# Latents in a decoder kernel: the first four tiles' roots, scaling and turns move between the projections

## The chip, the cores and the metric

The kernel runs on one core of a Trainium2 chip. The metric is device time in microseconds (us), the median of several executions. A core has five engines that run side by side, each through its own list of instructions: TensorE (PE; its weight loads are listed as PEld), VectorE (DVE), ScalarE (ACT), GpSimd (POOL) and SyncE (SP, which only issues transfers here). TensorE writes its results to PSUM, from where VectorE or ScalarE takes ("evicts") them to on-chip memory.

## What is computed

The program is two layers of a decoder on x of shape (4, 1024, 256): attention, cross attention and a feed-forward block in each. The change is in the fifth of the six blocks, the cross attention of the second layer, in which the 1024 rows of x are the latents and a context of 77 rows is attended to together with them. All arithmetic is float32. Cut to what matters:

```python
def _L1_xattn_ref(x, latents, mask, ...):          # x: context (4, 77, 256), latents (4, 1024, 256)
    def rmsnorm(x, gamma):
        n = jnp.linalg.norm(x, axis=-1, keepdims=True) * x.shape[-1] ** (-0.5)
        return x / jnp.maximum(n, RMS_EPS) * gamma
    xn = layernorm(x, ln_x_g, ln_x_b)
    ln = layernorm(latents, ln_l_g, ln_l_b)
    q = ln @ W_q
    kv = jnp.concatenate([xn @ W_kv, ln @ W_kv], axis=1)
    k, v = (kv[..., :INNER], kv[..., INNER:])      # 4 heads of 64
    q, k, v = (to_heads(q), to_heads(k), to_heads(v))
    qn = rmsnorm(q, q_gamma) * SCALE
    kn = rmsnorm(k, k_gamma)
    sim = jnp.einsum('bhid,bhjd->bhij', qn, kn)
    attn = softmax(where(mask, sim, -max))
    out = jnp.einsum('bhij,bhjd->bhid', attn, v)
    return out @ W_out + b_out                     # added to the latents
```

## The kernel before

The class `Latents` works through the four batches one after the other. A batch has 1024 rows: 8 tiles (`NTB`) of 128 rows. Its preparation is a generator, `projected(b, got)` (from line 2005), that stops at each `yield`; what lies between two yields is called a piece here.

In the first eight pieces, one for each tile t, TensorE makes `pk` (keys and values, 512 columns, line 2020) and `pq` (queries, 256 columns, line 2022). ScalarE copies the keys to `k` and the queries to `q` and squares both into `sq` (lines 2024, 2025, 2027, 2028). VectorE copies the values to `v` (line 2026) and sums the squares of each head into `sums[:, t]` (line 2029). `q` lies in a buffer that the trace calls `xn`.

The ninth piece takes the reciprocal root of all 64 sums of a partition: `inverse_rms` (line 1960, then `rsqrt`, lines 86 to 94), thirteen VectorE instructions in a chain: a scaling, three that make a first guess, and three Newton rounds of three. The queries' half is copied to `rq` (line 2040), which later scales the scores. Pieces ten and eleven scale four tiles of keys in place (`times_rms`, line 1967) and turn four tiles of queries; pieces twelve and thirteen turn the keys. To turn four tiles (`turn`) is eight transposes on TensorE (line 2047), four to a PSUM tile, and two evictions of 128x512 by ScalarE (line 2048) into `qT` or `kT`, with gamma as the scale. After that a fourteenth call ends the generator.

All of this takes its PSUM tiles from one pool, `ps_t`, with two buffers of the name `pt`, used in turn: a matmul into a `pt` waits until the tile two before it has been evicted by all its readers. The attention's transposes and projections use the same two buffers. The scores have three buffers of their own (`sc0`, `sc1`, `sx`).

In this stage the order of instructions on TensorE, ScalarE and VectorE is the order in which the program writes them (`manual_schedule`).

Batch 0 is prepared before any attention: its pieces alternate with those of the context (`of_context`), which has a reciprocal root of its own for 16 sums (issued after the fifth piece, in the first round of the loop over `range(12)`), a scaling of its keys (after the seventh piece) and four small turns of its keys (lines 1998 and 2001, issued after pieces ten to thirteen).

Batches 1 to 3 are prepared during the attention of the batch before. A batch's attention has 16 steps: four pairs of row tiles, times two pairs of heads, times two tiles. A step makes scores for two heads (`scores`, line 2072 and following; `nm` and `nx` are their maxima on VectorE), takes the exponentials on ScalarE (lines 2099 and 2105), turns the step before's weights (`turned`, lines 2122 and 2129), does pieces of earlier weighing and output work (`weighed`, `project_out`), and then calls `next(coming)` once. `coming` is `ahead(b + 1, got)`: at its k-th call it does piece k + 1 of `projected(b + 1)`, and from k = 9 on also a piece of `rows(b + 2)`, the layer norm and turning of the batch after next (statistics, root and normalization on VectorE, transposes on TensorE). For batch 1 the rows come first, so that its pieces start in the fourth step of batch 0's attention, with two calls at k = 12; its rows' pieces are doubled from k = 11 on.

## Time and profile before

| what | value |
|---|---|
| median of 3 runs | 4187.01 us (4185.9 to 4192.95) |
| the profiled execution's own time | 4175.77 us |
| its span, first to last instruction | 4174.0 us |
| mean granted TensorE clock | 0.977 |

The span is what the profile shows of one execution, and the execution's own time is 1.8 us longer. The changed block runs from about 2858 us to 3562 us of the span. In parts, with the busy time of each engine:

| from, to (us) | what runs | PE | DVE | ACT | clock |
|---|---|---|---|---|---|
| 2856 to 2872 | batch 0 and context prepared | 14.28 | 5.31 | 4.87 | 1.00 |
| 2872 to 2885 | the same | 11.22 | 7.64 | 5.64 | 1.00 |
| 2885 to 2902 | the same, to the first scores | 13.50 | 8.72 | 10.22 | 0.84 |
| 2902 to 3060 | attention of batch 0, batch 1 prepared | 142.63 | 105.82 | 83.05 | 0.95 |
| 3060 to 3225 | about batch 1 | 147.72 | 104.04 | 84.58 | 0.98 |
| 3225 to 3395 | about batch 2 | 152.67 | 100.11 | 88.19 | 0.97 |
| 3395 to 3565 | about batch 3, and the next block's statistics | 155.21 | 123.75 | 82.92 | 1.00 |

Lines of a timeline give start, length, engine, line of the kernel, operation, what is written and read, the shape and the count; in brackets stands the time for which the engine was idle before it, and what released it. Matmuls are merged into runs, and their ends are modelled. A row of the windows gives the stretch, its length, the busy time of the engines with the number of instructions, the granted clock (1.00 is full), the share of the transfer engines and GB/s.

### The profile page before, as it was taken

How to read it: one execution, taken by the hardware profiler on the slowest of the kernel's cores; microseconds unless marked ns; L12 is line 12 of the kernel's file. 1: busy time of each engine (PE TensorE's matmuls, PEld its weight loads, DVE VectorE, ACT ScalarE, POOL GpSimd, SP SyncE). 2: the span in 40 equal slices, each digit the busy share in tenths (PEclk: the TensorE clock that was granted, in tenths of full speed). 3: DMA queues.
4: the chain of work that ended last, by engine and by line, in shares of the span. 5: the costliest groups of instructions: out<-in, count | busy, mean ns of one | idle time of the engine just before them, and what ended most of it. 6: DMA issues, size and time to landing. Idle time of an engine off the chain costs nothing.

```text
span 4174.0 us, 58034 instructions
## 1 busy us (share of the span) xinstructions
PE 3933.5 (94%) x22350; PEld 2831.1 (68%) x22350; DVE 2967.8 (71%) x5464; ACT 1629.3 (39%) x2616; POOL 1018.8 (24%) x1218
## 2 busy tenths in 40 slices
PE   8899668999999999999999999998989899899999
PEld 6644336888788887888878877884555555557765
DVE  6646688888878888788878888875567567543324
ACT  4334465334333443333433333433555455112220
POOL 1100001333333343333333333331000000012215
PEclk9989889999999999999999999998999999899999
DMA  2010000000000000000000000000000000302213
GB/s 68 1 41 1 1 23 1 1 1 1 1 1 1 1 1 1 1 1 1 1 1 1 1 1 1 1 1 28 1 1 1 1 1 11 115 25 63 65 41 110
DMA packets 50906, 64.30 MB, mean 15 GB/s; under 512 B 8557, under 2 KB 44769, under 8 KB 50625
## 3 DMA queue, kind: packets, MB, share of 16 engines
q1 hardware_dynamic: 44145, 42.81, 3.2%
q0 software_dynamic: 6480, 17.70, 1.5%
q8 instruction: 181, 2.97, 0.3%
q14 instruction: 100, 0.82, 0.1%
HBM read 42.80 MB, written 17.69 MB: 14 GB/s over the span
## 4 chain that ended last, share of the span: by engine, by line
PE 68%; DVE 15%; ACT 1%; issue 1%; ACTq 0%; DVEq 0%
PE sc L1578 35%; PE po L1607 5%; PE ph L2652 4%; PE ph L2580 3%; PE sc L2072 3%; DVE mx L1586 3%; DVE nm L2085 3%; DVE pr L1596 3%; PE po L2154 2%; PE po L2682 2%; PE po L2567 2%; PE pt L2020 1%; DVE prT L2123 1%; PE pt L2122 1%; DVE km L1568 1%
## 5 line engine op out<-in xcount | busy, mean ns | idle before, releaser
L1578 PE MATMUL sc<-qT,km 128*128 128x256 f32 x8064 | 1789.8, 381 | 8.8 <-DVE pr L1596 8.8
L1578 PEld LDWEIGHTS sc<-qT,km 128*128 128x128 f32 x8064 | 1518.6, 190 | 272.3 <-issue 60.9
L1599 ACT ACTIVATE pr<-pr,zb 128x1024 f32<-128x1024 f32 x512 | 588.2, 1149 | 1316.8 <-DVE pr L1596 1302.1
L1588 POOL PARTITION_ALL_REDUCE top<-mx x512 | 544.6, 1064 | 1449.7 <-DVE mx L1586 1449.7
L1586 DVE TENSOR_REDUCE mx<-sc 128x256 f32<-128x1024 f32 x512 | 625.7, 1222 | 309.2 <-PE sc L1578 306.5
L1596 DVE TENSOR_TENSOR pr<-sc,top 128x1024 f32<-128x1024 f32 x512 | 622.0, 1215 | 0.0
L1568 DVE SCALAR_TENSOR_TENSOR km<-kT,w_L_attn_conv_w,km 128x512 f32<-128x512 f32 x504 | 380.9, 759 | 24.7 <-ACT km L1555 20.0
L1591 POOL COPY tops<-top 32x256 f32<-32x256 f32 x512 | 269.3, 526 | 32.7
L1607 PE MATMUL po<-pr,v 128*32 128x256 f32 x4096 | 249.3, 384 | 0.0
L2085 DVE TENSOR_REDUCE nm<-sc 128x1 f32<-128x1024 f32 x128 | 156.2, 1220 | 79.4 <-PE sc L2072 79.4
L2099 ACT ACTIVATE pr<-sc,nb,rq 128x1024 f32<-128x1024 f32 x128 | 155.1, 1212 | 127.9 <-PE pt L2129 109.5
L1607 PEld LDWEIGHTS po<-pr,v 128*32 128x32 f32 x4096 | 120.4, 110 | 109.6 <-issue 43.2
L2652 PE MATMUL ph<-wgu,xnT 128*128 x568 | 179.8, 459 | 0.6 <-ACT xnT L2641 0.6
L1555 ACT ACTIVATE km<-kT,w_L_attn_conv_w 128x512 f32<-128x512 f32 x252 | 173.5, 706 | 5.4 <-PE po L1361 5.4
L2659 DVE TENSOR_TENSOR xnT<-ph,xnT 128x352 f32<-128x352 f32 x71 | 37.3, 525 | 187.7 <-ACT xnT L2658 187.7
L2137 POOL COPY rb<-rinv 128x256 f32<-128x256 f32 x32 | 12.8, 400 | 629.3 <-DVE rinv L2113 388.3
L2122 PE MATMUL pt<-ident,pr 128*128 128x128 f32 x1024 | 144.4, 282 | 20.4 <-DVE X L2173 11.2
L2122 PEld LDWEIGHTS pt<-ident,pr 128*128 128x128 f32 x1024 | 113.0, 143 | 45.6 <-issue 18.8
L2072 PE MATMUL sc<-kT,qT 64*128 64x512 f32 x512 | 135.0, 627 | 2.9 <-ACT pr L2099 2.9
L2652 PEld LDWEIGHTS ph<-wgu,xnT 128*128 128x128 f32 x568 | 102.3, 190 | 46.0 <-ACT xnT L2641 0.9
L2154 PE MATMUL po<-prT,v 128*64 128x256 f32 x1024 | 132.6, 391 | 0.2 <-DVE oT L2161 0.2
L2123 ACT COPY prT<-pt 128x512 f32<-128x512 f32 x128 | 69.0, 589 | 146.1 <-PE pt L2122 146.1
(515 smaller groups left out, 4845.9 us busy)
## 6 DMA issues: line engine op xcount, KB each, us to landing
yrows<-xnT SPq DMA_DIRECT2D x71, 128.0 KB, 1.7
X<-in_x SPq DMA_DIRECT2D x8, 512.0 KB, 7.3
out<-X SPq DMA_DIRECT2D x8, 512.0 KB, 3.1
wgu<-in_L_ffn_w_gate SPq DMA_DIRECT2D x8, 352.0 KB, 6.6
wgu<-in_L_ffn_w_up SPq DMA_DIRECT2D x8, 352.0 KB
raw<-in_L_ffn_w1T SPq DMA_DIRECT2D x4, 512.0 KB, 3.5
raw<-in_L_ffn_w2T SPq DMA_DIRECT2D x4, 512.0 KB, 3.8
xrows<-xn SPq DMA_DIRECT2D x2, 1024.0 KB, 5.1
```

Source lines behind the costliest of these rows:

```text
L1568: nc.vector.scalar_tensor_tensor(km, keys, weight, km, ALU.mult, ALU.add)
L1578: nc.tensor.matmul(sc[:, j, :], km[:, c, bass.ts(j, P)], qT[:, c, bass.ts(i, Q2)], start=(c == 0), stop=(c == 1),)
L1586: nc.vector.tensor_reduce(mx, sc.rearrange("p j q -> p q j"), AX.X, ALU.max)
L1588: nc.gpsimd.partition_all_reduce(top, mx, P, bass_isa.ReduceOp.max)
L1591: nc.gpsimd.tensor_copy(tops[n][rows, i % (NQ, 2)[n], :], top[rows])
L1596: nc.vector.tensor_tensor(pr, sc, top.unsqueeze(1).to_broadcast([P, KT, Q2]), ALU.subtract)
L1599: nc.scalar.activation(pr, pr, AF.Exp, bias=zb[:, h : h + 1])
L1607: nc.tensor.matmul(po[32 * e : 32 * e + 32, :], v[:, n * KT + j, 4 * g + e, :], prs[e][:, j, :], start=(j == 0), stop=(j == KT - 1),)
L2072: nc.tensor.matmul(sc[e][:, bass.ts(n, 512)], lhsT[at], kT[at, d, bass.ts(n, 512)], start=True, stop=True,)
L2085: nc.vector.tensor_reduce(nm, sc[e], AX.X, ALU.max, negate=True)
L2122: nc.tensor.transpose(pt[:, n, :], pr[e][:, bass.ts(j + n, P)], net.ident)
L2652: nc.tensor.matmul(ph[:, k, :F], s["xT"][:, c, :], wgu[:, bass.ds(s["e"] * GU + (2 * c + k) * F, F)], start=(c == 0), stop=(c == 1),)
```

## The change

`inverse_rms`, the copy to `rq` and the scaling of the keys are put into a function `finish(t)` that does them for four tiles; it is called once for tiles 0 to 3 and once for tiles 4 to 7. `turn` stays as it was and is defined earlier. Inside the loop over the tiles, the first `finish` stands before the projection of tile 5, the turn of the first four tiles' queries before that of tile 6, and the turn of their keys before that of tile 7. After the loop come `finish()` for the last four tiles, the turn of their queries and the turn of their keys, a piece each. The generator has eleven pieces before its end where it had thirteen. Nothing else changes: the calls in `ahead` and in the loop over `range(12)` stay, with the last of them finding nothing to do.

```diff
                 qT = p2.tile([P, 2, S], F32, name="qT")
                 kT = p2.tile([P, 2, S], F32, name="kT")
+                rq = p2.tile([P, NTB, H], F32, name="rq")
+
+                def turn(src, dst, t, g):
...
+                def finish(t=4):
+
+                    flat = sums[:, t : t + 4].rearrange("p t s h -> p (t s h)")
+                    r = inverse_rms(flat, P, 4 * 2 * H, "rs").rearrange(
+                        "p (t s h) -> p t s h", s=2, h=H
+                    )
+                    nc.vector.tensor_copy(rq[:, t : t + 4], r[:, :, 0, :])
+                    times_rms(k[:, t : t + 4], r[:, :, 1, :], P)
+
                 for t in range(NTB):
+                    if t == 5:
+                        finish(0)
+                    if t == 6:
+                        turn(q, qT, 0, gq)
+                    if t == 7:
+                        turn(k, kT, 0, gk)
                     pk = ps_t.tile([P, 512], F32, name="pt")
                     pq = ps_t.tile([P, 512], F32, name="pt")
...
                     yield
-                flat = sums.rearrange("p t s h -> p (t s h)")
-                r = inverse_rms(flat, P, NTB * 2 * H, "rs").rearrange(
-                    "p (t s h) -> p t s h", s=2, h=H
-                )
-                rq = p2.tile([P, NTB, H], F32, name="rq")
-                nc.vector.tensor_copy(rq, r[:, :, 0, :])
+                finish()
                 yield
-
-                def turn(src, dst, t, g):
...
-                for t in range(0, NTB, 4):
-                    times_rms(k[:, t : t + 4], r[:, t : t + 4, 1, :], P)
-                    turn(q, qT, t, gq)
-                    yield
-                for t in range(0, NTB, 4):
-                    turn(k, kT, t, gk)
-                    yield
+                turn(q, qT, 4, gq)
+                yield
+                turn(k, kT, 4, gk)
+                yield
                 got.append((qT, kT, v, rq))
```

More of the change, by code (lines that the diff above doesn't have):

```diff
@@ L2014, in projected @@
                 kT = p2.tile([P, 2, S], F32, name="kT")
-                for t in range(NTB):
+                rq = p2.tile([P, NTB, H], F32, name="rq")
+                def turn(src, dst, t, g):
+                    for d in range(2):
+                        pt = ps_t.tile([P, 4, P], F32, name="pt")
+                        for j in range(4):
+                            nc.tensor.transpose(pt[:, j, :], src[:, t + j, bass.ts(d, P)], net.ident)
+                        nc.scalar.activation(
+                            dst[:, d, t * P : (t + 4) * P], pt.rearrange("p j q -> p (j q)"),
+                            AF.Copy, scale=g,
+                        )
[3 more added lines that the diff above has]
+                        "p (t s h) -> p t s h", s=2, h=H
+                    )
+                    nc.vector.tensor_copy(rq[:, t : t + 4], r[:, :, 0, :])
+                    times_rms(k[:, t : t + 4], r[:, :, 1, :], P)
+                for t in range(NTB):
+                    if t == 5:
[4 more added lines that the diff above has]
+                        turn(k, kT, 0, gk)
                     pk = ps_t.tile([P, 512], F32, name="pt")
@@ L2034, in projected @@
                     yield
-                flat = sums.rearrange("p t s h -> p (t s h)")
-                r = inverse_rms(flat, P, NTB * 2 * H, "rs").rearrange(
-                    "p (t s h) -> p t s h", s=2, h=H
-                )
-                rq = p2.tile([P, NTB, H], F32, name="rq")
-                nc.vector.tensor_copy(rq, r[:, :, 0, :])
-                yield
-                def turn(src, dst, t, g):
-                    for d in range(2):
-                        pt = ps_t.tile([P, 4, P], F32, name="pt")
-                        for j in range(4):
-                            nc.tensor.transpose(pt[:, j, :], src[:, t + j, bass.ts(d, P)], net.ident)
-                        nc.scalar.activation(
-                            dst[:, d, t * P : (t + 4) * P], pt.rearrange("p j q -> p (j q)"),
-                            AF.Copy, scale=g,
-                        )
-                for t in range(0, NTB, 4):
-                    times_rms(k[:, t : t + 4], r[:, t : t + 4, 1, :], P)
-                    turn(q, qT, t, gq)
-                    yield
-                for t in range(0, NTB, 4):
-                    turn(k, kT, t, gk)
-                    yield
+                finish()
+                yield
+                turn(q, qT, 4, gq)
+                yield
+                turn(k, kT, 4, gk)
+                yield
                 got.append((qT, kT, v, rq))
```

## The prediction

> **What bounds the kernel now.** I began with the page's busy shares and its chain of waits. They say that the whole span leans on TensorE, and that the changed stage (lines 2020 to 2173) is a small part of it.

> ```profile
> PE 3933.5 (94%) x22350; PEld 2831.1 (68%) x22350; DVE 2967.8 (71%) x5464; ACT 1629.3 (39%) x2616; POOL 1018.8 (24%) x1218
> ...
> PE 68%; DVE 15%; ACT 1%; issue 1%; ACTq 0%; DVEq 0%
> ```

> Next the timeline of the stage's start (columns: start, length, engine, line, operation, count, idle before it and its releaser). From 2858 to 2901 us batch 0 is projected while no attention runs yet, so no other work covers a wait. The lines are the place where the context's reciprocal root runs, and the end of this prologue:

> ```profile
> 2881.33 0.69 DVE L2029 TENSOR_REDUCE sums<-sq 128x8 f32<-128x512 f32 x1 [0.44 <-ACT sq L2028]
> ...
> 2881.93 0.16 DVE L1960 TENSOR_SCALAR ss_c<-ss_c 77x16 f32<-77x16 f32 x1
> ...
> 2884.27 0.41 DVE L2026 COPY v<-pt 128x256 f32<-128x256 f32 x1
> ...
> 2884.54 1.98 PE L2020 MATMUL pt<-w_L_xattn_W_kv,xnT 128*128 128x512 f32 x4 [0.75 <-ACT sq L2028]
> ...
> 2890.93 1.09 PE L2047 MATMUL pt<-ident,xn 128*128 128x128 f32 x8 [0.35 <-DVE v L2026]
> ...
> 2892.03 0.20 DVE L1960 TENSOR_SCALAR sums<-sums 128x64 f32<-128x64 f32 x1
> ...
> 2895.06 0.18 DVE L2040 COPY rq<-ri_rs 128x32 f32<-128x32 f32 x1
> 2895.15 2.35 DVE L1967 TENSOR_TENSOR k<-k,ri_rs 128x1024 f32<-128x1024 f32 x2
> ...
> 2896.51 1.82 PE L2047 MATMUL pt<-ident,k 128*128 128x128 f32 x8 [1.79 <-DVE k L1967]
> ```

> The reader is to see three things. VectorE does its instructions in the written order: the copy of `v` for tile 5 stands behind thirteen small instructions of the context's root and starts only at 2884.27, though its projection was done before. TensorE, which has two PSUM buffers `pt`, waits for that copy's buffer. And the turns of `k` wait for the root and the scaling (1.79 us).

> Then the granted clock in stretches of 2 us, and one attention step of batch 1:

> ```profile
> 2894.00:2896.00 2.00, 0.65 (x5) 0.26 (x3) 1.85 (x6) 1.67 (x4) 0.00 (x0) 1.00 0.01 4
> 2896.00:2898.00 2.00, 1.49 (x8) 1.44 (x8) 1.50 (x2) 0.48 (x1) 0.00 (x0) 0.67 0.00 0
> 2898.00:2900.00 2.00, 1.67 (x8) 1.18 (x7) 0.00 (x0) 1.55 (x4) 0.00 (x0) 0.50 0.00 0
> ```
> ```profile
> 3147.89 0.42 DVE L2026 COPY v<-pt 128x256 f32<-128x256 f32 x1 [1.98 <-ACT sq L2025]
> ...
> 3149.98 1.22 DVE L2085 TENSOR_REDUCE nm<-sc 128x1 f32<-128x1024 f32 x1 [0.53 <-PE sc L2072]
> ```

> Column nine of the first fence is the clock: it falls to 0.50 after the wait. In the second, VectorE has 1.98 us free before `v` in this step. The stage's windows are PE-busy 90 to 91%: a step is TensorE's work plus under 1 us of waits.

> **The change, part by part.** Counts: the root (13 VectorE instructions) and the copy to `rq` now run twice a batch, so 14 more small VectorE instructions a batch; scalings, turns and their evictions stay as many. No DMA and nothing on POOL or SP is added. The generator has 12 pieces instead of 14.

> *Length of one `finish`.* The thirteen take 2.34 us at 16 elements (2881.93 to 2884.27) and 3.03 at 64 (2892.03 to 2895.06). 32 elements are not in the trace; linear between the two gives 2.57. With 0.09 to the scaling (2895.06 to 2895.15) and half of 2.35 for four tiles, one `finish` is 3.84 us; bounds 3.6 and 4.3 with either end.

> *Prologue.* `finish(0)` is written ahead of tile 5's projection, so it lands between the context's root and the copy of `v` for tile 5: that copy moves from 2884.27 to about 2888.1. Queued behind it are `sums` of tile 5 and all later VectorE work; TensorE's next instruction, now the turn of `q`, needs the buffer. Nothing covers it: **+3.84**. TensorE, not queued behind other work, then idles from 2883.8, the end of tile 5's projection, to 2888.4, 4.6 us. The two turns set between projections cost what one cost before, 1.43 us each (from 2890.93 to 2892.36, when the next user of a `pt` started after ScalarE's eviction): **+2.86**; at 1.09 each if evictions hid, 2.2. At the end only one turn of each kind is left. Before, from the first turn of `q` to the first scores 10.52 us passed (2890.93 to 2901.45). After: 1.10 to the root's start, 3.84 for `finish(4)`, 0.18 to TensorE (k's first scaling ends 2896.33, TensorE starts 2896.51), then 2.34 from the second turn of `k` to the scores as now (2899.11 to 2901.45), and two context turns that used to lie in waits and now come behind it, 0.79 each by ScalarE's eviction of one: 9.04. **−1.5**. The end keeps a root of its own: 32 elements take nearly as long as 64, and 3.84 us stay between the last sum and `k`. Lastly the clock. After 1.79 us of wait it was 0.67, 0.50, 0.50 and 0.63 in four stretches of 2 us, a loss of up to 3.4 us, and eight transposes took 1.82 instead of 1.09. After 4.6 us I expect the same; part of it falls into eviction waits. From 0 to 3.4, I take **+1.0**, nearer to the 0.73 of the eight transposes than to the whole dip. Prologue: 3.84 + 2.86 − 1.5 + 1.0 = **+6.2**; bounds 3.5 (3.6 + 2.2 − 1.5 − 0.8 for `k` at full clock) and 9.1.

> [...]

> *Attention steps.* One `nx` reduction (line 2087) marks each step. Bare periods, read in the last batch, go 7.75, 8.23, 8.61, 9.50 in turn; a projection adds 2.6 to 2.8, a turn alone 0.86 to 1.17, the old root 0 to 0.35. For batch 2's pieces: (a) `finish(0)` with 1.98 us free ahead of `v`: from 3145.83 it ends 3149.7, then `v` and `sums`, so `nm` starts 0.75 late, and the addition to X that TensorE waits for later in the step (0.53) with it: +0.75. (b) The turn of `q` ahead of tile 6's projection: TensorE gets there at 3155.70, ScalarE's exponentials end at 3156.84, its eviction takes 0.69, so the projection starts 1.9 late instead of 1.0. (c) The turn of `k` ahead of tile 7: at 3166.55, ScalarE free at 3167.03, 1.4. (d) `finish(4)`: 0.2, since the root's 0.26 us of slack before `nm` goes. (e) the second turns, beside statistics of the next rows: 1.16 (1.66 before; the scaling that delayed `nm` by 0.5 is gone) and 1.02. After 6.4, before 1.66 + 1.02 + 0.86 + 1.02 = 4.6: **+1.8**. Batch 3, without next rows, by the same pieces with 1.0 for each second turn: 6.25 against 4.07 (1.17 + 1.01 + 0.87 + 1.02), **+2.2**. Batch 1, whose pieces start at the fourth step: `finish(0)` has 4.06 us free, 0; turns 1.7 and 1.9; `finish(4)` 1.15 (0.35 before); second turns 1.02 and 1.16; then a step bound by VectorE's rows 1.34 and, without its turn, 3.4: 11.7 against 8.9 (0.35 + 1.02 + 1.66 + 1.34 + 4.54), **+2.8**. Stage: **+6.8**. Bounds: −1.0 if the eviction waits and the late `nm` are absorbed and only the 0.5s remain, +10.5 at 3.5 a batch (where a held `v` also holds the next step's turns).

> *Sum:* 6.2 + 6.8 = **+13.0 us**, 0.31%. The profiled execution's own time is 4175.8 (span 4174.0 and 1.8 around it), so 4188.8 for a like one; it lay 11.2 below the median of the runs, 4187.0, from which the forecast is **4200.0**.

> **Rivals.** *Only the prologue pays.* TensorE is idle about 9% in the steps, and the four turns' work is the same; if their waits vanish in this slack, +5.3 (without the clock) to +6.2 is left: 4192.7. Against it: a turn alone already costs its whole 1.0 in every kind of step. *Faster: the clock stays up.* Place: 2896 to 2935, where the clock was low in three dips worth 3.4, 5.1 (2906 to 2918) and 1.8 us. If VectorE took `v` ahead of `finish(0)` there is no hold: 2.86 − 1.5 = +1.4, and with first scores reached without a cold start, up to −10.2, and −0.5 twice in the steps: about −10, 4177. It decides from the point where TensorE never waits over 1.8 us between tile 5 and the scores. Against it: the context's thirteen went ahead of `v` in just this way, and `finish(4)` leaves a wait of about 3 us before `k`. *Worse: the hold repeats.* If the late `v` holds TensorE in every batch as in the prologue, 9.1 + 10.5 = +19.6: 4206.6. For: `v` frees one of only two buffers. Against: scores, which need none, come between.

> **How the numbers follow.** Forecast 0.62 (its own range 4195.5 to 4205), only the prologue 0.18, faster 0.12, the hold repeats 0.08. Time: the likeliest, 4200.0. Range: lowest sum 3.5 − 1.0 = +2.5 less the 1.1 by which a run lay under the median, 4188; highest 4206.6 and some of the 5.9 that a run lay above it, 4210. Within 0.2% (8.4 us, about what a measurement of this kernel can tell from no change) lie the second case and a little of the first: 0.20. Faster is the third, 0.12; slower the rest, 0.68.

> **What would show it.** Right: two thirteens of 32 elements per batch; the copy of `v` for tile 5 of batch 0 about 4 us after its projection, and TensorE idle 4 to 5 us before its first `q` turn; first scores about 6 us later after the stage's start; steps with turn and projection 1.4 to 1.9 longer than with projection alone. Wrong: `v` before the small instructions, or a gap between first scores and last step that stays at its length; then the stage's 6.8 falls, and a full clock from 2900 on would turn the sign.

## The result and the profile after

Before 4190.6 us, after 4205.6 us (medians of nine runs each): a ratio of 1.0038, interval 1.0029 to 1.0046, so 12 to 19 us slower. The forecast was 13.0 us more, and 4200.0 us in a range of 4188 to 4210. Measured again (run e11 below) the ratio was 1.0037 (1.0023 to 1.0052).

The spans of the two profiled executions are 4174.0 and 4201.8 us, 27.8 apart and thus further than the medians; of this, 11.6 us lie between tile 5's projection in batch 0 and the end of the attention, as worked out below. The page of the changed kernel, engines and chain of waits:

```profile
span 4201.8 us, 58077 instructions
...
PE 3947.6 (94%) x22338; PEld 2835.9 (67%) x22350; DVE 2975.1 (71%) x5520; ACT 1628.0 (39%) x2616; POOL 1018.8 (24%) x1218
...
PE 67%; DVE 15%; ACT 2%; issue 1%; another core or an unknown queue 0%; ACTq 0%; DVEq 0%
```

VectorE has 56 instructions more (5464 before), four batches of 14, and is busy 7 us longer. ScalarE, GpSimd and the weight loads count as before; 12 matmul records fewer stand beside as many weight loads, so they are missing from the trace and not from the work. TensorE still sets the end. So the page tells nothing of where the time went; the timeline does. First the prologue of the changed kernel. The projection of tile 5 starts at 2885.76 here (2880.95 before); line 2021 is a turn's transposes, 2022 its eviction, 2047 and 2049 the projections, 2053 the copy of `v`:

```profile
2888.91 0.39 ACT L2055 ACTIVATE sq<-pt 128x256 f32<-128x256 f32 x1
...
2889.08 0.17 DVE L1960 TENSOR_SCALAR sums<-sums 128x32 f32<-128x32 f32 x1
...
2889.35 0.66 PE L2021 MATMUL pt<-ident,xn 128*128 128x128 f32 x4 [0.75 <-ACT sq L2055]
...
2890.05 0.69 ACT L2022 ACTIVATE qT<-pt,w_L_xattn_q_gamma 128x512 f32<-128x512 f32 x1 [0.75 <-PE pt L2021]
...
2890.79 0.66 PE L2021 MATMUL pt<-ident,xn 128*128 128x128 f32 x4 [0.78 <-ACT qT L2022]
...
2892.22 3.51 PE L2047 MATMUL pt<-w_L_xattn_W_kv,xnT 128*128 128x512 f32 x4 [0.78 <-ACT qT L2022]
2892.97 0.42 DVE L2053 COPY v<-pt 128x256 f32<-128x256 f32 x1
...
2905.35 0.17 DVE L2033 COPY rq<-ri_rs 128x16 f32<-128x16 f32 x1
2905.44 1.22 DVE L1967 TENSOR_TENSOR k<-k,ri_rs 128x1024 f32<-128x1024 f32 x1
2906.80 1.94 PE L2021 MATMUL pt<-ident,k 128*128 128x128 f32 x8 [3.45 <-DVE k L1967]
```

The reader is to see that the copy of `v` is as late as forecast (2892.97, 3.89 us after the new root began), but that TensorE does not wait for it. The turn of `q` begins 0.27 us after the root, as soon as ScalarE has squared the queries of tile 5. That is the end of use of the *other* `pt`, the one of the queries. Its second half and then tile 6's projection wait each for the eviction of the half before (0.78 us, twice): all three go through one buffer, while the late `v` holds the other. Behind it, the projection takes 3.51 us in place of 1.98: the clock, granted at 0.63 and 0.51 in the two stretches of 2 us from 2892 on. And at the end stands a wait for `k` of 3.45 us where one of 1.79 stood.

For the steps, the period from one `nx` to the next, for the steps of batch 2's attention in which batch 3 is prepared (differences of the starts of line 2087, after 2095):

| step's piece | before | after | difference | forecast |
|---|---|---|---|---|
| tile 5, after: first root ahead | 12.07 | 12.73 | +0.66 | +0.75 |
| tile 6, after: turn of q ahead | 10.52 | 12.29 | +1.77 | +1.9 |
| tile 7, after: turn of k ahead | 10.85 | 12.29 | +1.44 | +1.4 |
| root, after: second root and scaling | 8.61 | 9.03 | +0.42 | +0.2 |
| q turned (first; after: second) | 10.67 | 10.24 | −0.43 | −0.2 |
| q turned (after: second of k) | 8.76 | 8.77 | 0 | 0 |
| k turned (after: nothing) | 9.10 | 8.07 | −1.03 | −0.87 |
| k turned (after: nothing) | 9.63 | 8.60 | −1.03 | −1.02 |

The sum is +1.81 (forecast +2.2). The other 8 steps of the batch agree within 0.02 us. One step with a turn ahead of a projection, in batch 1's attention of the changed kernel:

```profile
3170.31 0.20 ACT L2113 ACTIVATION_READ_ACCUMULATOR pr<-sx,nb,rq 128x1 f32 x1
3170.41 1.26 ACT L2022 ACTIVATE qT<-pt,w_L_xattn_q_gamma 128x512 f32<-128x512 f32 x2
3171.14 1.98 PE L2047 MATMUL pt<-w_L_xattn_W_kv,xnT 128*128 128x512 f32 x4 [0.67 <-ACT qT L2022]
```

ScalarE comes to the evictions only when its exponentials are done (3170.41), and the projection waits 0.67 us for the first of them. A turn that is followed by scores, which have buffers of their own, has no such wait: in the same profile the second turns begin at 3204.21 and 3213.22 and the scores 1.27 and 1.02 us later, with no wait of TensorE ahead of them, where the projection behind this turn starts 1.76 us after the turn's start.

### The profile page after: what moved, and what is told of

Read it like the earlier page. It is cut to its first block, busy times and chain, and to the rows that moved or that the text cites. A ratio compares the mean times of both kernels' runs of the same rounds, so it can differ in the third digit from the quotient of the medians.

```text
span 4201.8 us, 58077 instructions
## 1 busy us (share of the span) xinstructions
PE 3947.6 (94%) x22338; PEld 2835.9 (67%) x22350; DVE 2975.1 (71%) x5520; ACT 1628.0 (39%) x2616; POOL 1018.8 (24%) x1218
## 4 chain that ended last, share of the span: by engine, by line
PE 67%; DVE 15%; ACT 2%; issue 1%; another core or an unknown queue 0%; ACTq 0%; DVEq 0%
PE sc L1578 35%; PE po L1607 5%; PE ph L2660 4%; PE ph L2588 3%; PE sc L2080 3%; DVE mx L1586 3%; DVE nm L2093 3%; DVE pr L1596 3%; PE po L2162 2%; PE po L2690 2%; PE po L2575 2%; PE pt L2047 1%; DVE prT L2131 1%; DVE km L1568 1%; PE pt L2130 1%
## 5 line engine op out<-in xcount | busy, mean ns | idle before, releaser
L2130 PE MATMUL pt<-ident,pr 128*128 128x128 f32 x1024 | 143.7, 281 | 20.7 <-DVE X L2181 11.6
```

The source lines that it names most:

```text
L2130: nc.tensor.transpose(pt[:, n, :], pr[e][:, bass.ts(j + n, P)], net.ident)
```

## The experiments

Each run gives a ratio to the kernel before on the same chip, and its profile three stretches: **P**, from the start of tile 5's projection in batch 0 to the first scores (and to the first `nx`); **A**, from the first to the last `nx`; **R**, from the last `nx` to the end of the span. The first two profiles give P 20.50 (24.66), A 644.43, R 623.96 before and P 24.88 (29.84), A 650.84, R 635.36 after.

**e1 and e2: each half of the change alone.**

```diff
-                    if t == 5:
+                    if b == 0 and t == 5:     # e1; e2: b > 0
                         finish(0)
...
+                if b == 0:                    # e1; e2: b > 0
                     finish()
...
+                else:                         # as before
```

> The change for batch 0 alone; batches 1 to 3 as before. Theory (prologue and steps each pay): from the start of tile 5's projection to the first scores 24.9 us as in the changed kernel (20.5 before), and the attention, first to last nx, as before, 644.4 us within 1.5; time about 5 us over before. Rival (the loss is the steps' alone, the prologue's 4.4 was the clock's luck): 20.5 to 22 us there and a time within 2 us of before.

Ratio 1.0018 (1.0009 to 1.0027); P 23.35 (28.31), A 644.12, R 624.02.

> The change for batches 1 to 3 alone; batch 0 as before. Theory: prologue 20.5 us as before; in batches 2 and 3 the steps with the turn before a projection 12.3 us each (10.5 and 10.85 before), 4.3 us lost and 2.5 won back in a batch; attention 648 to 651 us against 644.4; time 4 to 6 us over before. Rival (the steps have slack and the time comes from the prologue): attention within 1 us of 644.4 and a time within 2 us of before.

Ratio 1.0026 (1.0014 to 1.0037); P 20.14 (24.67), A 654.38, R 627.30. Both halves cost time, 7.5 us (4 to 11) and 10.9 us (6 to 15) by the ratios, so both rivals fall. These are more than the 5 and the 4 to 6 us expected. A is longer than expected, by two dips of the clock of 1.6 us each. P in e1 is 1.5 under the changed kernel's first and the same as in its second profile (e5 below), in which the granted clock was 1.00 through tile 6's projection.

**e3: the first root behind tile 5's copy of `v` and its sums.**

```diff
-                    if t == 5:
-                        finish(0)
...
                         sums[:, t], sq.rearrange("p s (h d) -> p s h d", h=H), AX.X, ALU.add
                     )
+                    if t == 5:
+                        finish(0)
```

> The first root and scaling moved behind tile 5's copy of v and its sums on VectorE, all else as in the changed kernel. Theory (the late v leaves one PSUM buffer for the turn of q, which costs 1.44 us and lets the clock fall, 1.5 us): the two halves of the first turn of q follow each other without a wait for the eviction, the turn takes 1.4 us instead of 2.9, the projection after it 2 us instead of 3.5, and from tile 5's projection to the first scores 21.5 to 23 us instead of 24.9. In the steps nm comes up to 3 us later in the step of tile 5: 0.5 to 2.5 us more per batch. Rival (the loss is the turns' own TensorE work and evictions): still 24 to 25 us in the prologue.

P 22.32 (26.77): as expected; R 626.17. The turn of `q` before tile 6, in e3's timeline:

```profile
2884.32 0.41 DVE L2051 COPY v<-pt 128x256 f32<-128x256 f32 x1
2884.59 1.09 PE L2021 MATMUL pt<-ident,xn 128*128 128x128 f32 x8 [0.75 <-ACT sq L2053]
...
2885.28 1.26 ACT L2022 ACTIVATE qT<-pt,w_L_xattn_q_gamma 128x512 f32<-128x512 f32 x2 [0.75 <-PE pt L2021]
2886.02 1.98 PE L2045 MATMUL pt<-w_L_xattn_W_kv,xnT 128*128 128x512 f32 x4 [0.34 <-ACT qT L2022]
```

With `v` copied in time both buffers are free: eight transposes in one run, 1.43 us to the projection instead of 2.87. The same order in the steps is bad: the root now delays `nm` by 3.3 us in each batch and the steps behind it (14.64, 15.35 and 15.35 us in place of 11.4, 12.7 and 12.7 in the changed kernel), A is 662.28, the ratio 1.0071 (1.0057 to 1.0084). The best place in the prologue is the worst in the steps; I had expected 0.5 to 2.5 us a batch, and against the changed kernel these steps lost 2.3 us in the first of the three batches and 4.3 and 4.4 in the others.

**e4: only batch 0 changed, its first root as in e3, all turns after the loop.**

```diff
+                    if b == 0 and t == 5:
+                        finish(0)             # behind the sums, as in e3
...
+                if b == 0:
+                    finish()
+                    yield
+                    turn(q, qT, 0, gq)
+                    yield
+                    turn(q, qT, 4, gq)
+                    yield
+                    turn(k, kT, 0, gk)
+                    yield
+                    turn(k, kT, 4, gk)
+                    yield
+                else:                         # as before
```

> Batch 0 alone: first root and scaling behind tile 5's VectorE work, all four turns after the loop as before; batches 1 to 3 as before. Theory (only the wait for k behind the last root is worth removing, and turns belong into it): TensorE never waits over 1 us for k, from tile 5's projection to the first scores 17.5 to 19 us against 20.5, clock at 1.00 until the first scores; time 2 to 4 us under before. Rival (VectorE's 3.8 us ahead of the copies for tiles 6 and 7 hold TensorE by as much): 20 to 22 us, no gain.

P 18.75 (21.91), A 642.44, R 624.13; ratio 0.9990 (0.9981 to 1.0000), so it is the only version at or under the kernel before. The end of its prologue:

```profile
2893.57 1.22 DVE L1967 TENSOR_TENSOR k<-k,ri_rs 128x1024 f32<-128x1024 f32 x1
2894.10 0.77 ACT L2001 ACTIVATE kcT<-pt,w_L_xattn_k_gamma 64x154 f32<-64x154 f32 x2
2894.26 1.32 PE L2021 MATMUL pt<-ident,k 128*128 128x128 f32 x8 [0.34 <-ACT qT L2022]
...
2896.36 1.33 PE L2021 MATMUL pt<-ident,k 128*128 128x128 f32 x8 [0.32 <-ACT kT L2022]
...
2898.07 1.99 PE L2096 MATMUL sc<-kT,qT 64*128 64x512 f32 x8
```

TensorE waits for evictions alone, never for `k`: three turns fill the time of the last root, and its clock was 1.00 until 2904 us.

**e7 and e8: the roots alone, and one turn alone.**

```diff
 e7: finish(0) ahead of tile 5 as in the change; all turns after the loop
 e8: one root for eight tiles after the loop, as before
+                    if t == 6:
+                        turn(q, qT, 0, gq)
...
                     times_rms(k[:, t : t + 4], r[:, t : t + 4, 1, :], P)
-                    turn(q, qT, t, gq)
+                    if t:
+                        turn(q, qT, t, gq)
```

> The root in two halves, the first ahead of tile 5 as in the changed kernel, but all turns after the loop. Theory: in the prologue the projection of tile 6 finds one buffer and its second half waits for the late v, about 2.2 us; the end has no wait for k, as in the run with the early root: 20.5 to 21.5 us from tile 5's projection to the first scores. In the steps 0.66 for the late nm and 0.43 for the second half, less 0.4 to 0.9 where the scaling stood: attention 644 to 646 us. Rival (a root of its own for four tiles costs its 2.6 us in every batch): attention over 650 us.

P 20.32 (23.48), A 643.75, R 634.60; ratio 1.0004 (0.9995 to 1.0014). TensorE's projections of tile 6 in e7:

```profile
2889.77 1.98 PE L2043 MATMUL pt<-w_L_xattn_W_kv,xnT 128*128 128x512 f32 x4 [0.75 <-ACT sq L2051]
2893.86 1.13 PE L2045 MATMUL pt<-w_L_xattn_W_q,xnT 128*128 128x256 f32 x4 [2.11 <-DVE v L2049]
```

Here the late `v` is waited for, but one tile later and for 2.11 us: the first projection has the free buffer, the second has none. So the hold exists, and what decides is how many buffers the work behind it needs. Two roots a batch by themselves cost nothing measurable (2 us less to 6 more by the interval).

> Only the turn of the first four tiles' queries is moved ahead of tile 6's projection; root and scaling once for eight tiles, as before. Theory: prologue 20.5 + 1.4 = 21.9 us, since the turn lay before in a wait for the root; in the steps 1.77 paid and 1.02 won back in a batch, attention 645.5 to 647.5 us; time 3 to 4 us over before. Rival (a turn costs the same wherever it stands): 20.5 us and 644.4 us.

P 22.07 (26.08), A 647.68, R 629.17; ratio 1.0018 (1.0008 to 1.0027). The steps of tile 6 take 12.28 us (10.52 before) in batches 2 and 3. Of what was to be won back, 1.02 and 1.17 came in the first and third batch and nothing in the second, where VectorE's scaling and statistics set the step (11.16 with and without the turn). A dip of the clock in that batch, 1.4 us, brings A slightly over its expected 645.5 to 647.5. The ratio says 7.5 us (3 to 11) where 3 to 4 were expected. Roots in two halves are harmless within e7's interval; the turns between projections are what costs.

**e6: in the steps VectorE evicts the first turns.**

```diff
+                        if t == 0 and b > 0:
+                            nc.vector.tensor_scalar(
+                                dst[:, d, : 4 * P], pt.rearrange("p j q -> p (j q)"), g, None, ALU.mult
+                            )
+                        else:
```

> In batches 1 to 3 VectorE, not ScalarE, evicts the first turns; all else as in the changed kernel. Theory (the projection behind a turn waits for the eviction of its buffer, and that waits for ScalarE's exponentials): the steps with the turn of q, 12.28 us, fall to 11.8 to 12.0; those with the turn of k, where ScalarE was nearly free, stay at 12.2 to 12.3. Rival (it is TensorE's own transposes, 1.09 us, and the semaphores): both stay within 0.1.

P 23.36 (27.80), A 651.60, R 629.93. The steps of tile 6 fall from 12.28 to 12.02, those of tile 7, where ScalarE was nearly free, go from 12.28 to 12.34; ratio 1.0030 (1.0019 to 1.0042). ScalarE's lateness is thus worth some 0.3 us of the 1.77: the 0.26 won, and the 0.06 by which VectorE's eviction is the slower one. The other 1.5 is the turn itself and the wait for whichever engine evicts it.

**e5, e9, e10 and e11: what lies outside the stage.** These are the two kernels unchanged.

> The changed kernel once more, for a second profile. Theory (of the 27.8 us between the two spans only the stage's 11.6 belong to the change; the 11.4 behind the stage are waits that this one execution had): from the last nx to the end 624 to 628 us, not 635; from tile 5's projection to the first nx 28 to 30 us, attention 647 to 652, with steps that differ from the first profile only by dips of the clock of about 1.5 us each. Rival (the program's new length moves the last block's instructions so that they wait): again 635 us behind the last nx.

P 23.35 (28.31), A 651.13, R 630.53: neither 624 to 628 nor 635.

> The kernel before once more, for a second profile. Theory (the stretch behind the stage and the start of the stage vary from execution to execution whatever the kernel): prologue 20.5 us and attention 643 to 645 us as before, but behind the last nx up to 635 us, not 624.0 again. Rival (624.0 belongs to the kernel before, and the change or the longer program costs 3 to 11 us there): 624.0 within 0.5.

P 20.05 (24.67), A 644.76, R 624.02: here the rival was right, and the theory had no support yet. R has been 624.0 to 624.1 in e1, e4 and here, all with the later batches as before, and 626.2 to 635.4 in the changed kernel and in all its other parts: that looked like a cost of the change. So one pair was run together on one chip:

> The kernel before, profiled on the same chip as the run beside it. Theory (what lies behind the stage depends on the chip and not on the kernel): the two kernels' stretches from the last nx to the end agree within 1.5 us, be it at 624 or at 630 to 635. Rival (the change costs there): 624.0 here and 626 to 635 in the changed kernel.

P 20.41 (24.65), A 644.42, R 628.26.

> The changed kernel on the same chip. Theory: from the last nx to the end within 1.5 us of the run beside it; from tile 5's projection to the last nx 10 to 12 us longer than there (28.3 to 29.8 and 650 to 651 against 24.7 and 644 to 645), and a time 10 to 15 us over before. Rival (the change costs 3 to 11 us behind the stage as well): 2 us or more above it there.

P 24.79 (29.74), A 650.00, R 627.97; ratio 1.0037 (1.0023 to 1.0052). In this pair R is the same for both kernels within 0.3 us. From e10's timeline, TensorE in the expert loop:

```profile
3770.21 2.63 PE L2652 MATMUL ph<-wgu,xnT 128*128 x8 [0.32 <-issue]
3804.51 2.63 PE L2652 MATMUL ph<-wgu,xnT 128*128 x8 [0.31 <-issue]
```

A wait that no semaphore ends, every 34.3 us, the time of eight blocks. With these waits the loop (first to last start of its line 2652) takes 297.5 us here, and 297.5 to 298.3 in e5 to e8, in e11 and in the first profile after; without them it takes 294.15, in the first profile before, in e9 and in e1 to e4. The kernel before has them in one of its three profiles, and e1 to e4, each with a part of the change, lack them, so it is not the change alone that decides; what does, no run shows.

Of the 11.4 us by which R differed between the first two profiles, these waits are 4.1. The 5.6 us behind the loop did not come again in the changed kernel: from the loop's last matmul to the end it took 150.3 us there, but 146.0 and 145.0 in e5 and e11, and the kernel before took 144.7 to 145.6. The last 1.7 us are one dip of the clock more between the last `nx` and the loop. So no fixed cost of 3 to 11 us lies behind the stage. But six of the eight profiles with a change in the later batches lost 1.6 to 3.3 us to such dips there (all but e8 and e11), and none of the five without; that a part of it belongs to the change is thus not excluded.

What does belong to the change is the stage: from tile 5's projection to the last `nx` 669.1, 669.4 and 669.1 us before and 680.7, 679.4 and 679.7 after, 10.0 to 11.6 us. The ratios say 15 (12 to 19 in the first measurement, 10 to 21 in e11). The difference of some 4 us is inside the second interval, not inside the first, and in each of the seven other versions the ratio lies above the stage's difference too, by 0.7 us in e4 to 9.8 in e3. So a part of it is probably real. Where it lies, behind the stage or before it (which began at 2857.7 to 2862.3 us of the span before and 2860.5 to 2861.9 after), stays open.

## Why the prediction held, and which step of it was wrong

The total (+13.0, own range 8.5 to 18 over before) holds the measured 15.0, and the direction and the two places were right. The traces account for 10.0 to 11.6 of these in the stage, so the hit of the total says less than the steps do. By its steps:

- *VectorE works in the written order, and the copy of `v` comes 3.84 us late.* Shown: 3.89 in the first profile, and e3 takes it away. One `finish` was forecast at 3.84, with 2.57 for the thirteen; they took 2.68.
- *TensorE needs that buffer, so +3.84 and 4.6 us of idling.* **Wrong.** I had taken the two `pt` buffers as used strictly in turn, and the description of the kernel says so too. The trace shows that the next tile got the buffer that became free first. The prediction's own lines of the kernel before show it too, and it read them wrongly: tile 6's projection starts at 2884.54, released by ScalarE's `sq`, while the copy of `v` ends only at 2884.68 (2884.27 and 0.41). TensorE idled 0.75 us before the turn of `q`, not 4.6, and the term measured 1.44 instead of 3.84 (the turn of `q` took 2.87 instead of 1.43), since three tiles had to pass through one buffer. e7 shows the hold itself where the work behind needs both: 2.11 us.
- *Turns between projections, 1.43 each.* Right for the turn of `k` (4.62 instead of 3.20 us from tile 6 to tile 7 in e5: 1.42); that of `q` is the 2.87.
- *The end wins 1.5.* Right: from the last projection to the first scores 13.71 before, 12.26 in e5. The wait for `k` stayed, and grew from 1.79 to 3.45, because turns that had filled it were gone. e4, which leaves them there, has no such wait.
- *The clock, 1.0 between 0 and 3.4.* Beyond what the kernel before loses there, it cost 1.5 before the first scores in the first profile and in e11, nothing in e5, and then 0.3 to 0.8 between the first scores and the first `nx`.
- *Prologue +6.2.* To the first scores, where the forecast ended its sum, 4.4 us in the first profile and in e11 and 2.9 to 3.3 in e5 (against the two profiles of the kernel before); to the first `nx` 5.2, 3.7 and 5.1. The hold was 2.4 too large, and where the sum came near all the same, a clock that cost more than the 1.0 made up for part of it. That is luck.
- *Steps +6.8.* 6.4, 6.7 and 5.6 us. Outside dips of the clock, the steps with a piece of the change lie within 0.5 us of their forecast. But two dips that were not forecast nearly cancel. In batch 2's pieces (−0.1, forecast +1.8) the kernel before loses 1.41 us in one step that the changed kernel does not lose. In batch 3's own attention, where nothing of the change runs and nothing was forecast, the changed kernel loses 1.64 us in the fourth step in all three profiles; the last section has that step. So the agreement of the sum is in part luck too.

Of the rivals, that only the prologue pays fell with e2, that the clock stays up with the first profile, and that the hold repeats in each batch with the steps, where scores come between. That "a full clock from 2900 on would turn the sign" was not seen in the changed kernel: no profile of it had such a clock. In e5 the clock stayed up through the projections and the sign stayed, but from 2902.3 on, 4.2 us before the first scores, it was halved for 20.5 us. e4 had the clock up to 2904 us, but its turns stand elsewhere too, so it does not price the clock alone.

## What to carry to other kernels

Work moved off the end of a chain must not be the work that filled a wait there: first see what the waiting engine does meanwhile (here the wait for `k` grew from 1.79 to 3.45 us). A turn with an eviction is cheap ahead of work that has its own PSUM buffers (here 1.02 to 1.27 us from its start to the scores), and costs its eviction as well ahead of work that shares them (1.43 to 1.76 us to the projection). Before a buffer wait is priced, count the buffers that the work behind needs and take the one that becomes free first, not the next in turn (here the turn of `q` began at 2889.35, and the `pt` that `v` is copied from was free only at 2893.39).

## What was not expected of the hardware

After a wait of TensorE of nearly the same length (1.77 and 1.78 us) the granted clock stayed at 1.00 in one kernel and fell to 0.50 in the other. The fourth step of the last batch has the same wait in both kernels, first before, then changed:

```profile
3450.09 0.44 PE L2129 MATMUL pt<-ident,pr 128*77 128x128 f32 x2 [1.77 <-DVE prT L2123]
```
```profile
3464.84 0.44 PE L2137 MATMUL pt<-ident,pr 128*77 128x128 f32 x2 [1.78 <-DVE prT L2131]
```

In the table by stretches the third figure from the end is the granted clock; the stretch after the wait in the kernel before:

```profile
3450.00:3452.00 2.00, 1.66 (x12) 0.90 (x12) 2.00 (x7) 1.47 (x3) 0.00 (x0) 1.00 0.00 0
3452.00:3454.00 2.00, 2.00 (x10) 0.69 (x8) 1.87 (x8) 0.62 (x4) 0.00 (x0) 1.00 0.38 129
```

And in the changed kernel:

```profile
3466.00:3468.00 2.00, 2.00 (x10) 0.88 (x12) 1.94 (x8) 1.37 (x6) 0.00 (x0) 0.50 0.00 1
3468.00:3470.00 2.00, 2.00 (x8) 0.76 (x8) 0.68 (x3) 0.00 (x0) 0.00 (x0) 0.65 1.02 344
```

The thirteen small VectorE instructions of a root take 2.34 us at 16 elements (2881.93 to 2884.27 before), 2.68 at 32 (2902.67 to 2905.35 after) and 3.03 at 64 (2892.03 to 2895.06 before): halving the elements saves about an eighth.
